# New weights and hand-over delays for the list scheduler of a two-layer attention kernel, and its weight products put under the scheduler

## The chip, the cores and the metric

The kernel runs on one core of one Trainium2 chip. The metric is device time in microseconds (us): the time of one execution of the whole program on that core. A second number, the span, comes from the profiler: from the first to the last instruction of one profiled execution. The core has five engines that work side by side, each through its own list of instructions in a fixed order: TensorE (PE in the profile, with PEld for its weight loads), VectorE (DVE), ScalarE (ACT), GpSimd (POOL) and SyncE (SP, which here only starts transfers). An instruction waits on semaphores for what it needs; while it waits, everything behind it on its engine waits too.

## What is computed

The input x has 8 batches of 64 x 16 positions with 128 channels, so 1024 tokens per batch. There are two layers.

```
# layer 0, per batch: 8 heads over all 1024 tokens
scores = einsum('bhlfc,bhmgc->bhlfmg', q, k) / sqrt(128)
a = softmax(scores, axis=4)          # over m (64)
a = softmax(a, axis=5)               # over g (16)
z1 = layernorm(a @ v @ wo + bo + x)
y  = layernorm(relu(z1 @ w1 + b1) @ w2 + b2 + z1)

# layer 1, per batch
Wi = einsum('bnd,ed->bne', norm(y), W)
s[i,j] = sum_d v[d] * tanh(Wi[j,d] + Wi[i,d])      # 1024 x 1024 x 128 tanh values
y = y + softmax(s, axis=-1) @ norm(y)
# then a recurrence over the 1024 tokens: y_t = sigmoid(wx_t + y_(t-1) @ V), added to y
```

The matrix s is symmetric, so the kernel computes a little more than half of it: some 4.2 million tanh values in each of the 128 partitions.

## The kernel before

**Weights are folded.** For each of the 8 heads the kernel multiplies wq with wk (tile A) and wv with wo (tile Wvo), each 128 x 128, and works out two bias vectors, ub and zb. In the kernel before, this is written out ahead of the scheduled part (lines 775 to 793): all of A and Wvo in turn on PE (L779) with copies by DVE (L782), then ub (L788, L789), with zb (L792, L793) between, and a small mask `half` (L749 to L754). The four weight tensors are loaded into the first four stretches of 1024 elements of the big tile `th`; xT, the transposed tokens, is loaded by SP right behind the first of them.

**Then a planner writes the order.** Everything from the first head of batch 0 to the last row of layer 1 of batch 7 is not written in order; it is added to a `Plan`. Each entry names an engine (or several to choose from), an estimated duration in us, the keys that it reads and writes, and a due time `pri`. `Plan.emit` then simulates the engines: an entry becomes ready when what it depends on has ended and a delay has passed, and that delay depends on the engine that ran it (`LATENCY`, or `AGAIN` when the next one is on the same engine). At each step the entry with the earliest due time among those that can start within 0.15 us of the earliest start is emitted. So durations and delays never reach the chip; they decide the order of each engine's list, and, where an entry has a choice, the engine.

**Layer 0** (function `layer0`), per head and per tile of 128 queries: u = A x + ub (PE L909, eviction L913 or L915), values (L923, L865 or L867), scores (PE L948, 16 matmuls on 32-column strips), exp (ACT L956), sums over m (PE L965, DVE L970), reciprocal (DVE L977), spreading over the partitions (PE L982), division (DVE L990). Two such tiles make a pair: second exp (ACT L1024), sums over g (DVE L1027), reciprocal (DVE L1030), division (POOL L1039), transposes (DVE L1042), attention times values (PE L1050), adding up in `zs` (DVE L1056, L1058). Then come a layer norm, the feed-forward part (L1098, L1102/L1104, L1112 to L1120) and another norm (L814, L815, L818, L819, L824), with affine steps on POOL (L1131, L1132).

**Layer 1** (function `group`): for some rows i of s, four interleaved columns c at a time, the sum Wi[j] + Wi[i] and its tanh are needed over all j. There are three ways:

- ACT alone: tanh of wiT with Wi[i] as the bias, one instruction per row (L1164, "direct");
- POOL adds the rows of a column in one instruction (L1174), and ACT later takes the tanh of all the group's added rows in one wide instruction (L1222);
- DVE adds, row by row with `tensor_scalar` and an accumulator that nobody reads (L1168), or, where a group has four or more rows, with one `tensor_tensor` (also L1174); the wide tanh follows too.

Which of them a group gets is the planner's choice, by which engine can start first. PE multiplies the rows with v into the PSUM tile `sa` (L1242), ACT takes the exp (L1338), POOL and DVE finish the diagonal block (L1344, L1348), and PE does the attention (L1371). The added rows lie in `th`, used as a ring: a POOL or DVE row can start only when PE has used up the rows that lay there.

**Interleaving**: layer 0 of batch b + 1 is planned beside layer 1 of batch b. Layer 0 of batch 0 has nothing beside it, and layer 1 of batch 7 has only the end of layer 0 of batch 7. After the plan come the normalisation over all batches, the recurrence (L1540 to L1561) and the output (L1570, L1572).

```
    LATENCY = {"PE": 0.6, "ACT": 0.5, "DVE": 0.4, "POOL": 0.6, "SP": 8.0}
    AGAIN = {"PE": 0.0, "ACT": 0.0, "DVE": 0.2, "POOL": 0.15, "SP": 8.0}
...
        def ready_at(n, e):
            t = max((began[d] for d in ops[n][7]), default=0.0)
            for d in ops[n][4]:
                t = max(t, done[d] + (self.AGAIN if by[d] == e else self.LATENCY).get(by[d], 0.0))
            return t
```

Of the kernel before, what the change touches and what calls it, by code (L numbers as in the profile page):

```python
# [15 lines left out]
P = 128  # L16
# [466 lines left out]
class Plan:  # L483
# [15 lines left out]
    LATENCY = {"PE": 0.6, "ACT": 0.5, "DVE": 0.4, "POOL": 0.6, "SP": 8.0}  # L499
# [134 lines left out]
def fast_path(ctx: ExitStack, tc: tile.TileContext, a: dict, fits):  # L634
# [79 lines left out]
    wkn = early(1, "wkn", nc.scalar)  # L714
    nc.sync.dma_start(out=xTs[0], in_=a["xt"][0])
    wvn = early(2, "wvn", nc.scalar)
    wo = early(3, "wo", nc.sync)
    bq = load(const, "bq", [P, H], nc.scalar)
# [21 lines left out]
    def by_token(x):  # L740
        return x.rearrange("p (r c) -> p c r", c=4)
# [6 lines left out]
    upper, moved = E_sb[:, 0, :], E_sb[:, 1, :]  # L748
    make_upper_triangular(nc, upper)  # L749
    nc.vector.scalar_tensor_tensor(upper, ident, -0.5, upper, ALU.mult, ALU.add)  # L750
    nc.vector.tensor_copy(half.rearrange("p (c r) -> p c r", c=4), by_token(upper))
    nc.vector.tensor_copy(moved.rearrange("p (c r) -> p c r", c=4), by_token(ident))
    nc.tensor.matmul(m0[:, :P], moved, half, start=True, stop=True)
    nc.vector.tensor_copy(half, m0[:, :P])  # L754
# [22 lines left out]
    for dst, left, right, pp in ((A, wqn, wkn, scs[0]), (Wvo, wvn, wo, scs[1])):  # L777
        for h in range(H):
            nc.tensor.matmul(pp[:, h * C : (h + 1) * C], left[:, h, :], right[:, h, :], start=True, stop=True)  # L779
            if h % 4 == 3:  # L780
                hs = slice(h - 3, h + 1)
                nc.vector.tensor_copy(  # L782
                    dst[:, hs, :], pp[:, (h - 3) * C : (h + 1) * C].rearrange("p (h c) -> p h c", c=C)
                )

    ub = tile_of(const, "ub", [P, H])
    for h in range(H):
        nc.tensor.matmul(m0[:, h : h + 1], wkn[:, h, :], bq[:, h : h + 1], start=True, stop=True)  # L788
    nc.vector.tensor_copy(ub, m0[:, :H])  # L789
    zb = tile_of(const, "zb", [P, 1])  # L790
    for h in range(H):
        nc.tensor.matmul(m1[:, 0:1], wo[:, h, :], bvn[:, h : h + 1], start=h == 0, stop=h == H - 1)  # L792
    nc.vector.scalar_tensor_tensor(zb, m1[:, 0:1], float(M), bo, ALU.mult, ALU.add)  # L793
# [10 lines left out]
    def layer_norm(src, kr, dst, kw, k, pri, on="POOL", then=None):  # L804
# [27 lines left out]
        add(("DVE", 1.9), statistics, r=[kr], w=[ks], pri=pri)  # L832
        add(("POOL", 1.5), power, r=[ks], w=[ks], pri=pri)
        add((on, 1.1 if on == "DVE" else 2.2), normalise, r=[kr, ks], w=kw, pri=pri, give=then)
# [24 lines left out]
    def copy(dst):  # L859
        def fn(e, bank):  # L860
            src = bank
            if len(dst.shape) == 3:
                src = bank[:, : dst.shape[1] * P].rearrange("p (t c) -> p t c", c=P)
            if e == "ACT":
                nc.scalar.activation(dst, src, AF.Copy)  # L865
            else:
                nc.vector.tensor_copy(dst, src)  # L867

        return fn

# [3 lines left out]
    def layer0(b):  # L874
# [17 lines left out]
        for n_part, part in enumerate(parts):  # L892
# [3 lines left out]
            for h in range(H):  # L896
# [8 lines left out]
                for s in range(2) if part is None else (part,):  # L905
# [11 lines left out]
                    through_bank(project, 0.9, [kx], biased, evict(0.75), [], [("u", h % 2, s)], L0, banks)  # L917
                for s in () if alone and n_part else range(2):

                    def values(bank, h=h, s=s):  # L920
# [7 lines left out]
                        values, 0.95, [kx], copy(vp[:, 4 * s : 4 * s + 4, :]), evict(0.68), [], [kvp + (s,)], L0, banks  # L928
                    )
                for qt in qts:  # L930
# [24 lines left out]
                    add(("PE", 1.74), scores, r=[kx, ("u", h % 2, qt // 4)], w=[kc], pri=L0, mode="groups")  # L955
                    add(("ACT", 0.98), lambda _, sc=sc, source=source: nc.scalar.activation(source, sc, AF.Exp, scale=SCALE),  # L956
                        r=[kc], w=[ksrc], pri=L0)
                    if by_pe:
# [15 lines left out]
                        through_bank(sums, 0.45, [ke], last_sums, ("DVE", 0.2), [], [k1], L0, banks, "groups")  # L974
# [17 lines left out]
                        add(("DVE", 0.2), first_inverse, r=[k1], w=[k1], pri=L0)  # L992
                        through_bank(spread, 0.3, [k1], divide, ("DVE", 1.22), [ke], [ke], L0, banks, "groups")
# [30 lines left out]
                    add(("ACT", 1.9), lambda _, e2=e2: nc.scalar.activation(e2, e2, AF.Exp), r=ks, w=ks, pri=L0)  # L1024
# [8 lines left out]
                    add(("DVE", 0.9), second_inverse, r=[k2], w=[k2], pri=L0)  # L1033
                    for q in range(2):
# [6 lines left out]
                        add(("POOL", 1.97), divide_again, r=[ke, k2], w=[ke], pri=L0)  # L1041
                        add(("DVE", 1.17), lambda _, e=e: nc.vector.transpose(e, e), r=[ke], w=[ke], pri=L0)  # L1042
# [17 lines left out]
                    for s in range(2):  # L1060
                        add(
                            ("PE", 1.74), lambda _, attend=attend, s=s: attend(s),
# [3 lines left out]
                    add(("DVE", 0.42), gather, r=[("bank", bank), kx], w=[kz + (qt // 4,)], pri=L0, give=bank)  # L1066

            L0 = b - 1 - SOON
            for qh in range(2) if part is None else (part,):
# [8 lines left out]
                add(("PE", 0.52), lambda _, bank=bank, z_tiles=z_tiles: z_tiles(bank()), r=[kz + (qh,)], w=[kb], pri=L0,  # L1078
# [4 lines left out]
                def affine1(e, bank, z1T=z1T):  # L1083
# [6 lines left out]
                    transposes([Xg[:, i, :] for i in range(4)]), 0.52, [kg], affine1, evict(0.75), [], [k1], L0, banks  # L1090
# [4 lines left out]
                for f in range(NFF):  # L1095
# [10 lines left out]
                    through_bank(hidden, 0.9, [k1], relu, evict(0.75), [], [kh[f]] if f % 2 == 0 else [kh[f]], L0, banks)  # L1106
# [20 lines left out]
                add(("PE", 5.4), outer, r=kh + [k1], w=[kb], pri=L0, take=bank, wait=[kg])  # L1127
# [6 lines left out]
                add(("POOL", 2.2), affine2, r=[kg], w=[kg], pri=L0)  # L1134
# [510 lines left out]
```

## Time and profile before

| what | value |
|---|---|
| median of 3 runs | 5300.66 us (5299.17 to 5303.35) |
| the profiled execution | 5300.69 us |
| its span | 5298.8 us |
| mean granted TensorE clock | 0.987 |
| instructions | 184474 |
| first tanh on ACT (L1164) | starts at 294.5 us |
| last exp on ACT (L1338) | starts at 5207.4 us |

The views used are: the page (busy time of each engine, the chain of work that ended last, the costliest groups), the table of busy time in stretches of the span, the groups by line, the timeline of one engine in a window, and the list of waits. In a group, "x1544" is the number of instructions and "mean ns" the mean recorded duration. Recorded durations of neighbours on one engine overlap a little, so where an exact price is wanted, it is taken from one start to the next. A PE matmul of the program shows as two instructions in the counts (x32 for the 16 matmuls of one score tile).

### The profile page before, as it was taken

The numbers are of one execution on the slowest core, as the hardware profiler recorded it, in microseconds if no ns is written. First come the engines' busy times: TensorE is split into PE (matmuls) and PEld (weight loads), VectorE is DVE, ScalarE is ACT, GpSimd is POOL, SyncE is SP. The second block draws the span as 40 slices with busy tenths as digits, with TensorE's granted clock in tenths as the row PEclk, the third lists the DMA queues.
The fourth block names the chain that finished last, engine by engine and source line by source line (L and its number), as shares of the span: only waits on it lengthen the run. The fifth ranks groups of instructions, "written<-read, shape, count | busy, mean of one in ns | idle before, by whom it ended". The sixth has DMA issues, their size and how long they took to land.

```text
span 5298.8 us, 184474 instructions
## 1 busy us (share of the span) xinstructions
PE 4915.6 (93%) x82181; PEld 3021.0 (57%) x82181; DVE 4739.3 (89%) x9090; ACT 4957.7 (94%) x3692; POOL 4437.4 (84%) x3064
## 2 busy tenths in 40 slices
PE   8899999999999999999999999999998999986567
PEld 6666656656665566556655566555664556552125
DVE  5788988889999999989998999989998999999886
ACT  4389999999999999999999999999999999999995
POOL 2366988679999899979999899989998989897992
PEclk9999999999999999999999999999999999998999
DMA  2000000000000000000000000000000000000001
GB/s 64 2 3 7 3 2 6 2 10 3 2 6 8 4 3 6 4 8 2 3 6 6 6 3 2 6 8 4 3 3 2 10 2 2 2 29 9 1 1 69
DMA packets 27669, 43.16 MB, mean 8 GB/s; under 512 B 2512, under 2 KB 19280, under 8 KB 26864
## 3 DMA queue, kind: packets, MB, share of 16 engines
q1 hardware_dynamic: 24832, 27.99, 1.6%
q8 instruction: 645, 10.57, 0.9%
q10 hardware_dynamic: 1872, 3.16, 0.2%
q14 instruction: 160, 1.31, 0.1%
q0 software_dynamic: 160, 0.13, 0.0%
HBM read 19.22 MB, written 12.06 MB: 6 GB/s over the span
## 4 chain that ended last, share of the span: by engine, by line
PE 67%; ACT 15%; DVE 11%; issue 5%; POOL 1%; DMA 0%; SPq 0%; ACTq 0%; DVEq 0%; POOLq 0%
PE sa L1242 23%; PE sc L948 14%; PE m L1050 13%; ACT th L1222 10%; DVE th L1168 3%; PE m L965 3%; ACT th L1164 3%; PE m L923 2%; PE m L982 2%; PE m L1371 2%; DVE stat_e L1027 2%; PE m L909 1%; DVE wx L990 1%; DVE th L1174 1%; PE m L1120 1%
## 5 line engine op out<-in xcount | busy, mean ns | idle before, releaser
L1174 POOL TENSOR_TENSOR th<-wiT 128x1024 f32<-128x1024 f32 (+55 forms) x2254 | 3255.7, 1479 | 308.9 <-PE sa L1242 270.3
L1222 ACT ACTIVATE th<-th 128x3210 f32<-128x3210 f32 (+57 forms) x1074 | 2926.5, 2767 | 27.0 <-DVE th L1174 15.6
L1242 PE MATMUL sa<-th,vpat 128*32 128x512 f32 (+33 forms) x24576 | 2045.9, 460 | 243.4 <-ACT th L1222 222.9
L1168 DVE TENSOR_SCALAR_CACHE_REDUCE th<-wiT 128x344 f32<-128x344 f32 (+61 forms) x2362 | 1945.8, 863 | 79.6 <-PE sa L1242 76.3
L1242 PEld LDWEIGHTS sa<-th,vpat 128*32 128x32 f32 x24576 | 715.7, 110 | 1186.2 <-issue 681.7
L1164 ACT ACTIVATE th<-wiT 128x501 f32<-128x501 f32 (+59 forms) x1544 | 1120.2, 797 | 16.1 <-PE sa L1242 14.9
L948 PE MATMUL sc<-xT,wx 128*32 128x256 f32 x16384 | 980.3, 380 | 2.2 <-issue 2.2
L1039 POOL TENSOR_TENSOR wx<-wx,stat_e 128x1024 f32<-128x1024 f32 x342 | 658.6, 1948 | 242.5 <-DVE stat_e L1030 153.9
L948 PEld LDWEIGHTS sc<-xT,wx 128*32 128x32 f32 x16384 | 549.9, 110 | 291.4 <-issue 45.5
L1050 PE MATMUL m<-wx 128*128 128x256 f32 x2400 | 563.1, 388 | 18.6 <-DVE stat_e L970 7.7
L1050 PEld LDWEIGHTS m<-wx 128*128 128x128 f32 x2400 | 449.6, 192 | 146.2 <-issue 45.6
L990 DVE TENSOR_TENSOR wx<-wx,m 128x1024 f32<-128x1024 f32 x330 | 396.9, 1206 | 38.6 <-PE m L982 36.8
L956 ACT ACTIVATE wx<-sc 128x1024 f32<-128x1024 f32 x342 | 340.3, 1022 | 93.8 <-PE sa L1050 35.9
L1042 DVE STREAM_TRANSPOSE wx<-wx 128x1024 f32<-128x1024 f32 x342 | 417.6, 1230 | 4.1 <-POOL wx L1039 3.6
L1039 POOL TENSOR_TENSOR e<-e,stat_e 128x1024 f32<-128x1024 f32 x170 | 327.1, 1946 | 97.6 <-DVE stat_e L1030 62.4
L1027 DVE TENSOR_REDUCE stat_e<-wx 128x128 f32<-128x2048 f32 x171 | 388.5, 2272 | 17.3 <-ACT wx L1024 16.1
L1024 ACT ACTIVATE wx<-wx 128x2048 f32<-128x2048 f32 x171 | 327.3, 1915 | 30.3 <-DVE wx L990 30.0
L982 PEld LDWEIGHTS m<-stat_e,ident 128*32 128x32 f32 x15808 | 224.0, 111 | 149.9 <-issue 76.7
L1050 PE MATMUL m<-e,wx 128*128 128x256 f32 x1184 | 278.6, 389 | 16.8 <-DVE e L1042 9.8
L1050 PEld LDWEIGHTS m<-e,wx 128*128 128x128 f32 x1184 | 221.7, 192 | 79.4 <-issue 21.7
L982 PE MATMUL m<-stat_e,ident 128*32 128x16 f32 x15808 | 229.2, 185 | 18.7 <-DVE stat_e L977 5.8
L1030 DVE RECIPROCAL stat_e<-stat_e 128x128 f32<-128x128 f32 x256 | 240.0, 938 | 0.2
(215 smaller groups left out, 4801.4 us busy)
## 6 DMA issues: line engine op xcount, KB each, us to landing
xT<-in_xt_dram SPq DMA_DIRECT2D x8, 512.0 KB, 3.4
th<-in_x_dram SPq DMA_DIRECT2D x8, 512.0 KB, 7.1
parked<-X SPq DMA_DIRECT2D x16, 256.0 KB, 2.3
xr<-parked SPq DMA_DIRECT2D x8, 512.0 KB, 6.9
parked_wx<-bT SPq DMA_DIRECT2D x14, 256.0 KB, 2.3
wx<-parked_wx SPq DMA_DIRECT2D x7, 512.0 KB, 3.7
out_dram<-ot ACTq DMA_DIRECT2D x8, 256.0 KB, 2.2
out_dram<-ot SPq DMA_DIRECT2D x8, 256.0 KB, 2.2
```

What stands on the lines that cost most here:

```text
L948: nc.tensor.matmul(sc[32 * a : 32 * a + 32, 256 * s : 256 * s + 256], u[:, rows], tokens[:, a], start=True, stop=True,)
L982: nc.tensor.matmul(bank[32 * a : 32 * a + 32, s * G : s * G + G], ident[:, 32 * s : 32 * s + 32], r1, start=True, stop=True,)
L990: nc.vector.tensor_tensor(quarters(e), quarters(e), r, ALU.mult)
L1027: nc.vector.tensor_reduce(r2, e2.rearrange("p q (m g) -> p q m g", g=G), AX.X, ALU.add)
L1039: nc.gpsimd.tensor_tensor(e3, e3, r2[:, q, :].unsqueeze(2).to_broadcast([P, M, G]), ALU.mult)
L1042: add(("DVE", 1.17), lambda _, e=e: nc.vector.transpose(e, e), r=[ke], w=[ke], pri=L0)
L1050: nc.tensor.matmul(bank()[:, :256], vp[:, t, :], keys[:, t], start=t == 0, stop=t == NT - 1)
L1164: nc.scalar.activation(rows(c)[:, r, :], wiT[:, i0 + begin[c] :], AF.Tanh, bias=w_i(c, r))
L1168: nc.vector.tensor_scalar(rows(c)[:, r, :], wiT[:, i0 + begin[c] :], w_i(c, r), 0.0, ALU.add, ALU.add, accum_out=next_unused())
L1174: eng.tensor_tensor(rows(c), wiT[:, i0 + begin[c] :].unsqueeze(1).to_broadcast(shape), w_i(c).unsqueeze(2).to_broadcast(shape), ALU.add,)
L1222: nc.scalar.activation(slot()[:, a:z], slot()[:, a:z], AF.Tanh)
L1242: nc.tensor.matmul(sa[32 * c : 32 * c + 32, s:s1], vpat[:, 31 - r0 - r : 63 - r0 - r], rows(c)[:, r, s - at0 - begin[c] : s1 - at0 - begin ...
```

## The change

Three things are changed.

1. The hand-over delays of the planner: PE 0.6 to 0.3, ACT 0.5 to 0.25, DVE 0.4 to 0.25, POOL 0.6 to 0.3 us. `AGAIN` stays.
2. The durations of some thirty kinds of entries. Most get smaller, some larger.
3. The weight products, ub, zb and `half` are no longer written out ahead of the plan. A new function adds them to it, in halves of four heads, with due times ahead of layer 0; they go through the PSUM banks m0, m1 and the two halves of sa, where the products had used the two score banks. Entries that use A, Wvo, ub, zb or `half` now name them as keys. The load of bq moves from behind wv to right behind wk on ACT's queue.

```
-    LATENCY = {"PE": 0.6, "ACT": 0.5, "DVE": 0.4, "POOL": 0.6, "SP": 8.0}
+    LATENCY = {"PE": .3, "ACT": .25, "DVE": .25, "POOL": .3, "SP": 8.0}
...
     wkn = early(1, "wkn", nc.scalar)
+    bq = load(const, "bq", [P, H], nc.scalar)
     nc.sync.dma_start(out=xTs[0], in_=a["xt"][0])
     wvn = early(2, "wvn", nc.scalar)
     wo = early(3, "wo", nc.sync)
-    bq = load(const, "bq", [P, H], nc.scalar)
...
-    for dst, left, right, pp in ((A, wqn, wkn, scs[0]), (Wvo, wvn, wo, scs[1])):
-        for h in range(H):
-            nc.tensor.matmul(pp[:, h * C : (h + 1) * C], left[:, h, :], right[:, h, :], start=True, stop=True)
...
+    def folded_weights():
+        first, later = -2.0, -1.36
+        for hs in (slice(0, 4), slice(4, 8)):
+            for name, dst, left, right, keys in (("A", A, wqn, wkn, (0, 1)), ("Wvo", Wvo, wvn, wo, (2, 3))):
+                def product(bank, left=left, right=right, hs=hs):
+                    for i, h in enumerate(range(hs.start, hs.stop)):
+                        nc.tensor.matmul(bank[:, i * C : (i + 1) * C], left[:, h, :], right[:, h, :], start=True, stop=True)
...
+                through_bank(
+                    product, 1.05, [("xn", k) for k in keys], kept, ("DVE", 0.6), [], [(name, hs.start)],
+                    later if hs.start else first if name == "A" else first + 0.6, four,
+                )
...
-        add(("DVE", 1.9), statistics, r=[kr], w=[ks], pri=pri)
-        add(("POOL", 1.5), power, r=[ks], w=[ks], pri=pri)
+        add(("DVE", 1.62), statistics, r=[kr], w=[ks], pri=pri)
+        add(("POOL", 1.27), power, r=[ks], w=[ks], pri=pri)
...
-                    through_bank(project, 0.9, [kx], biased, evict(0.75), [], [("u", h % 2, s)], L0, banks)
+                    through_bank(project, 0.96, [kx, ("A", h // 4 * 4), ("ub", h // 4 * 4)], biased, evict(0.66), [], [("u", h % 2, s)], L0, banks)
...
-                    add(("PE", 1.74), scores, r=[kx, ("u", h % 2, qt // 4)], w=[kc], pri=L0, mode="groups")
-                    add(("ACT", 0.98), lambda _, sc=sc, source=source: nc.scalar.activation(source, sc, AF.Exp, scale=SCALE),
+                    add(("PE", 1.73), scores, r=[kx, ("u", h % 2, qt // 4)], w=[kc], pri=L0, mode="groups")
+                    add(("ACT", 0.91), lambda _, sc=sc, source=source: nc.scalar.activation(source, sc, AF.Exp, scale=SCALE),
...
-                        through_bank(spread, 0.3, [k1], divide, ("DVE", 1.22), [ke], [ke], L0, banks, "groups")
+                        through_bank(spread, 0.28, [k1], divide, ("DVE", 1.13), [ke], [ke], L0, banks, "groups")
...
-                        add(("POOL", 1.97), divide_again, r=[ke, k2], w=[ke], pri=L0)
-                        add(("DVE", 1.17), lambda _, e=e: nc.vector.transpose(e, e), r=[ke], w=[ke], pri=L0)
+                        add(("POOL", 1.9), divide_again, r=[ke, k2], w=[ke], pri=L0)
+                        add(("DVE", 1.15), lambda _, e=e: nc.vector.transpose(e, e), r=[ke], w=[ke], pri=L0)
...
-            "POOL": lambda c: (0.27 + 1.62e-3 * k * (w - begin[c]), lambda: add_rows(nc.gpsimd, c)),
-            "DVE": lambda c: (k * (0.21 + 1.05e-3 * (w - begin[c])), lambda: [add_row(c, r) for r in rows_of])
+            "POOL": lambda c: (0.138 + 1.686e-3 * k * (w - begin[c]), lambda: add_rows(nc.gpsimd, c)),
+            "DVE": lambda c: (k * (0.193 + 0.966e-3 * (w - begin[c])), lambda: [add_row(c, r) for r in rows_of])
             if k < 4
-            else (0.15 + 1.04e-3 * k * (w - begin[c]), lambda: add_rows(nc.vector, c)),
+            else (0.138 + 0.957e-3 * k * (w - begin[c]), lambda: add_rows(nc.vector, c)),
...
-            lambda: ("ACT", sum(0.2 + 0.833e-3 * (z - a) for a, z in filled())) if filled() else None,
+            lambda: ("ACT", sum(0.1 + 0.833e-3 * (z - a) for a, z in filled())) if filled() else None,
```

The direct tanh of ACT keeps its weight, 0.18 + 0.833e-3 per element, and so do the products with v on PE, at 1.69e-3 per element. The kinds of instructions and the values that they compute are the same; what moves is their order, and which engine adds a row of Wi.

## The prediction, on record before the changed kernel ran

> **What bounds the kernel now.** I read the page first, then busy time by stretch, then the groups by line, the waits, and the timelines of ACT, DVE and PE. The page's first part and the stretches:
>
> ```profile
> PE 4915.6 (93%) x82181; PEld 3021.0 (57%) x82181; DVE 4739.3 (89%) x9090; ACT 4957.7 (94%) x3692; POOL 4437.4 (84%) x3064
> ```
>
> ```profile
> core 0: us, PE busy (x) PEld busy (x) DVE busy (x) ACT busy (x) POOL busy (x), PEclk, DMA share, GB/s
> 294.50:5207.40 4912.90, 4588.73 (x76851) 2768.33 (x76843) 4476.74 (x8615) 4808.11 (x3371) 4343.54 (x2995) 0.99 0.02 5
> 0.00:294.50 294.50, 257.02 (x4791) 189.32 (x4791) 205.25 (x313) 121.20 (x225) 90.39 (x64) 0.97 0.11 30
> 5207.40:5298.80 91.40, 69.83 (x547) 63.35 (x547) 57.27 (x164) 28.35 (x98) 3.44 (x6) 0.90 0.27 99
> 700.00:4600.00 3900.00, 3770.84 (x64319) 2331.75 (x64315) 3590.05 (x6798) 3819.04 (x2592) 3504.53 (x2426) 0.99 0.02 5
> ```
>
> 294.5 is the first tanh, 5207.4 the last exp of layer 1. Between them ACT is idle for 4912.9 - 4808.1 = 104.8 us of 4912.9 (2.1%): 81 of it between 700 and 4600, 3.4 behind 4600. That long middle is bound by ACT. PE's 97% is less than it looks: the chain of work prices one score tile at 1.73 us, a pair's attention at 3.65, one set of sums at 0.45; with all kinds counted out this way I get an estimate of some 4500 us where the page shows 4916, so PE has perhaps 8% in hand. The head (294.5 us) is a chain of PE and DVE. The tail (91.4 us) is the recurrence and the output.
>
> Who makes the tanh rows:
>
> ```profile
> L1174 POOL TENSOR_TENSOR th<-wiT 128x1024 f32<-128x1024 f32 (+55 forms) x2254 | 3255.7, 1479 | 308.9 <-PE sa L1242 270.3
> L1222 ACT ACTIVATE th<-th 128x3210 f32<-128x3210 f32 (+57 forms) x1074 | 2926.5, 2767 | 27.0 <-DVE th L1174 15.6
> L1168 DVE TENSOR_SCALAR_CACHE_REDUCE th<-wiT 128x344 f32<-128x344 f32 (+61 forms) x2362 | 1945.8, 863 | 79.6 <-PE sa L1242 76.3
> L1164 ACT ACTIVATE th<-wiT 128x501 f32<-128x501 f32 (+59 forms) x1544 | 1120.2, 797 | 16.1 <-PE sa L1242 14.9
> L1174 DVE TENSOR_TENSOR th<-wiT 128x768 f32<-128x768 f32 (+20 forms) x74 | 116.3, 1615 | 2.4 <-PE sa L1242 2.3
> ```
>
> Every element goes through ACT once, directly (L1164) or after POOL or DVE added it (L1222). What differs is ACT's fixed cost:
>
> ```profile
> 2046.50 0.88 ACT L1164 ACTIVATE th<-wiT 128x668 f32<-128x668 f32 x1
> 2047.24 2.47 ACT L1222 ACTIVATE th<-th 128x2698 f32<-128x2698 f32 x1
> 2049.59 1.04 ACT L956 ACTIVATE wx<-sc 128x1024 f32<-128x1024 f32 x1
> ```
>
> From start to start a direct row of 668 took 0.74 us and a wide one of 2698 took 2.35. At 0.83 ns an element (a wide row of 4096, 3.51 us from start to start, against one of 2280, 2.01) that leaves 0.185 us of overhead for a direct row and 0.11 for a wide instruction.
>
> **The sum, part by part.** The counts are from the two kernels' instruction lists; the prices from rows of before.
>
> *Rows move off ACT.* L1164 goes from 1544 to 1264 instructions, L1222 from 1074 to 1129; their elements together stay at 4,223,936, 177,136 change from direct to wide. ACT: -280 x 0.185 = -51.8 and +55 x 0.11 = +6.0, so **-45.8 us**. (By busy time less elements, 0.227 and 0.177 an instruction, it would be -53.8.) By batch: -224 and +48 in batches 1 to 6 (-36.1), the rest in the first and last. ACT does this work where it is 98 to 100% busy, so I count all of it.
>
> *They land on DVE and POOL.* DVE: +132 rows with 119,508 elements. A row of 1024 takes 1.20 us from start to start and one of 384 takes 0.53, so 0.13 + 1.05 ns an element: 17 + 125 = +142. The four-row adds go from 74 to 87, at 116.3/74 = 1.57 each: +20. POOL: +66 instructions with 52,804 elements, at 3255.7 us for 1,733,960 elements: +99. Nearly all lies between 700 and 4600. After the change that stretch would be 3900 - 36 = 3864 long, with ACT at 3783, DVE at 3590 + 155 = 3745 (97%), POOL at 3504 + 99 = 3604 (93%). The cover is DVE's idle time, 310 us now and 119 then; the price if it is not there is a rival below.
>
> *The order.* The planner's old weights were above what the trace shows, but not on every engine. Old minus new weight times count: DVE some 340 us (L1168 2362 x 0.07 = 167, L990 512 x 0.09 = 46, L970 36, the rest small), against 436 us that DVE idles in the middle; POOL some 220 (2254 x 0.08 + 512 x 0.07) of 569; ACT 169 (1074 x 0.1, 512 x 0.07, 256 x 0.1) of 105. PE's weights hardly change. So most of DVE's idle time is time in which the plan held it busy: it ran ahead and met PE, which was priced right.
>
> ```profile
> DVE zs L1058 <- PE m L1050: 72.6, 89, 3.8
> DVE stat_e L970 <- PE m L965: 35.6, 76, 1.8
> ACT wx L956 <- PE sc L948: 13.0, 21, 1.5
> ACT wx L956 <- PE m L1050: 11.6, 12, 2.4
> ```
>
> These waits (700 to 4600) are what a plan with true weights can fill. The delays don't become too short: in the timeline a DVE division ends at 2054.24 and ACT's second exp starts at 2054.27, and the planned 0.25 counts from about 0.1 before the recorded end. How ACT's idle of 104.8 us changes no row shows. Ends: the share behind 4600 (0.6%) over the whole middle is 27 us, a gain of 78; the share from 294.5 to 700 (20.4 of 405.5, 5%) is 243, a loss of 138. Nearest is the stretch from 1000 to 4000, 42.8 of 3000 or 1.4%, which gives 69; I go about a third of the way there: **-10 us**.
>
> *The products.* PE's list before the first u (L909):
>
> ```profile
> 12.34 2.05 PE L779 MATMUL sc<-th 128*128 128x128 f32 x8 [1.38 <-DMA th<-in_wo_dram]
> 14.18 3.41 PE L792 MATMUL m<-bvn_sb,th 128*128 128x1 f32 x16
> 20.49 3.57 PE L788 MATMUL m<-bq_sb,th 128*128 128x1 f32 x16 [0.55 <-DVE half L754]
> 24.32 2.08 PE L909 MATMUL m<-xT,A 128*128 128x512 f32 x2 [0.26 <-DVE ub L789]
> ```
>
> In the new list all of it still stands ahead of the first u, only `half` is gone: A's first half at 6.02 (2.07), ub's first half (1.8, if bq lands in time), then PE waits for wo until 12.34, then Wvo 2.05, A 2.05, Wvo 2.05, ub 1.8, zb 3.41: u at 23.7 in place of 24.32, **-0.6**. If bq lands as late as now (10.7 us after its issue), ub's first half moves behind 12.3 and u starts at 25.5, +1.2. SP's queue keeps its order; the loads of x behind it now wait for the products' readers, but only the bound check reads x, and nothing on the path waits for that. DVE's copies are the same in number. POOL first needs `half` at the first L1344, near 393 us. In the rest of the head the same 44 first exps, 21 second exps and 64 squares precede ACT's first tanh in both lists; I take 0 there, with -20 to +10, the idle time of PE in it (37 us) being the most there is.
>
> The Trainium skill has a rule against this change ("SBUF — State Buffer", section "Who interferes with whom"): a DVE instruction with two SBUF inputs and a GpSimd instruction that reads SBUF exclude each other for a whole instruction. The trace agrees:
>
> ```profile
> L1174 DVE TENSOR_TENSOR th<-wiT x74: 387/1134/10806, 394.9 to 4858.4; 128x1024 f32<-128x1024 f32 x8, 128x768 f32<-128x768 f32 x5, 128x828 f32<-128x828 f32 x3, 128x700 f32<-128x700 f32 x3
> ```
>
> One such add took 10.8 us. ACT waited 15.6 us for them (L1222's row above); 87 in place of 74 makes that 18.3, by which the sum would be 2.7 higher.
>
> Sum against the profiled execution, 5300.69 (span 5298.8; 1.9 lie around it; the median of the runs is 5300.66): 5300.7 - 45.8 - 10 - 0.6 = **5244 us**.
>
> **The rivals.**
>
> *PE is the bound in the middle*, and ACT's saving turns into waits for PE. For: the chain of work is 67% PE, and ACT's waits above are for PE. Against: PE's estimate above, and DVE and POOL rather than ACT idle most. Then only the first and last batch (-9.6) count, and -0.6: 5290. This is also the case in which the change does not do what it says. Chance 0.15.
>
> *DVE becomes the bound* (the other side). DVE has 3745 us of work between 700 and 4600. If its 310 us of waiting stay, because they are real hand-overs and not plan errors, the stretch takes 4055; the point from which it is slower than now is 3900 - 3745 = 155 us, half of the waits. With two thirds left: 3745 + 207 = 3952, +52, less 10 elsewhere: 5342. Against: 340 of 436 us are accounted for by weights. Chance 0.08.
>
> *The plan fits much better*: ACT's idle falls to the 27 us and the head gains 15: 5300.7 - 46 - 78 - 15 = 5162. For: waits for PE are most of ACT's idle time. Against: between 1000 and 4000 ACT already idles 1.4%. Chance 0.12.
>
> **The numbers.** 5244 has 0.65, for 5205 to 5280. The range 5180 to 5300 takes in that, most of the PE case and the nearer part of the good case. A measurement here tells about 0.2% (10.6 us) from no change. Faster by more than that: 0.65 + 0.12 + half of the PE case = 0.84; within it 0.08; slower 0.08.
>
> **What would show it.** Right: L1164 x1264 and L1222 x1129 with ACT busy near 4907; first tanh near 294; ACT's idle share in the middle at 2% or below; DVE's busy time up by some 160, and less waiting of L1058 and L970 for PE. Wrong: ACT's idle time well over 105 us (then look whether L956 waits for PE, or L1222 for DVE); a first tanh moved by over 10 us; L1168 or L1174 costing more apiece than before.

## The result, and the profile after

The changed kernel takes **5235.91 us** (median of 4 runs, 5231.66 to 5242.02) against 5302.01 for the kernel before in the same comparison (5299.17 to 5304.87): ratio 0.9883, 95% interval 0.9871 to 0.9895, or 62 us. Its profiled execution took 5237.67 us with a span of 5235.8. The sum of the prediction, 5244, is 8 us above it. Its terms are another matter, as the runs below show.

The first part of the page after:

```profile
PE 4889.8 (93%) x82181; PEld 3013.3 (58%) x82181; DVE 4885.7 (93%) x9372; ACT 4907.7 (94%) x3463; POOL 4536.1 (87%) x3130
```

ACT's busy time fell by 50.0 us (from 4957.7, predicted 4907), DVE's rose by 146.4, POOL's by 98.7. The groups of the tanh rows (the lines of the code have moved down by 27: L1164 is now L1191, L1222 L1249, L1168 L1195, L1174 L1201):

```profile
L1249 ACT ACTIVATE th<-th 128x3402 f32<-128x3402 f32 (+55 forms) x1129 | 3080.3, 2773 | 27.4 <-DVE th L1201 15.3
L1195 DVE TENSOR_SCALAR_CACHE_REDUCE th<-wiT 128x840 f32<-128x840 f32 (+60 forms) x2494 | 2088.7, 875 | 64.2 <-PE sa L1269 63.3
L1191 ACT ACTIVATE th<-wiT 128x596 f32<-128x596 f32 (+52 forms) x1264 | 913.1, 792 | 9.2 <-PE sa L1269 9.1
```

The counts are those of the prediction, and an instruction costs about what it cost (L1191 792 ns against 797, L1195 875 against 863, with other lengths in the mix). To see where the time went I cut both executions at the same three events: the first direct tanh, the last scores of layer 0 (L975, before L948), and the last wide tanh to start. Busy time by stretch, after, in the columns of the view shown for before (this is the second and the third stretch), and then the same two of the kernel before:

```profile
272.00:4624.50 4352.50, 4228.19 (x73095) 2636.02 (x73087) 4172.38 (x7856) 4248.52 (x2884) 3998.91 (x2746) 0.99 0.02 5
4624.50:5140.90 516.40, 339.95 (x3748) 125.47 (x3740) 448.53 (x1040) 510.63 (x264) 443.56 (x316) 0.96 0.03 9
```

```profile
294.50:4695.80 4401.30, 4252.88 (x73165) 2643.61 (x73161) 4041.38 (x7613) 4299.90 (x3085) 3915.51 (x2690) 0.99 0.02 5
4695.80:5204.30 508.50, 333.69 (x3662) 123.90 (x3654) 435.36 (x1003) 506.31 (x287) 428.03 (x306) 0.95 0.03 9
```

| stretch | before | after | difference | ACT idle | PE idle | DVE idle |
|---|---|---|---|---|---|---|
| head, to the first direct tanh | 294.5 | 272.0 | -22.5 | | 37.5 to 22.9 | |
| mixed, both layers side by side | 4401.3 | 4352.5 | -48.8 | 101.4 to 104.0 | 148.4 to 124.3 | 359.9 to 180.1 |
| last rows, no layer 0 left | 508.5 | 516.4 | +7.9 | 2.2 to 5.8 | 174.8 to 176.4 | 73.1 to 67.9 |
| end | 94.5 | 94.9 | +0.4 | | | |

(Idle is length less busy.) The head after, beside the prediction's row 0.00:294.50:

```profile
0.00:272.00 272.00, 249.14 (x4783) 187.00 (x4787) 207.51 (x314) 118.22 (x220) 90.14 (x64) 0.98 0.12 33
```

In the mixed stretch, 83% of the time, ACT lost 51.4 us of work and the stretch 48.8 us of length. That looks like a bound by ACT, as forecast. But PE also idles 24 us less, and is busy 25 us less with the same 82,181 instructions in the whole run; which of these is the cause, no view of these two kernels alone can say. The head's gain was not forecast.

### The profile page after: what moved, and what is told of

It is laid out like the page before. It is cut to its first block, busy times and chain, and to the rows that moved or that the text cites. A ratio compares the mean times of both kernels' runs of the same rounds, so it can differ in the third digit from the quotient of the medians.

```text
span 5235.8 us, 184559 instructions
## 1 busy us (share of the span) xinstructions
PE 4889.8 (93%) x82181; PEld 3013.3 (58%) x82181; DVE 4885.7 (93%) x9372; ACT 4907.7 (94%) x3463; POOL 4536.1 (87%) x3130
## 4 chain that ended last, share of the span: by engine, by line
PE 67%; DVE 14%; ACT 12%; issue 5%; POOL 2%; DMA 0%; ACTq 0%; DVEq 0%; POOLq 0%; SPq 0%
PE sa L1269 23%; PE sc L975 13%; PE m L1077 13%; ACT th L1249 9%; DVE th L1195 4%; PE m L992 3%; PE m L950 2%; PE m L1009 2%; PE m L1398 2%; DVE th L1201 2%; ACT th L1191 2%; DVE stat_e L1054 1%; PE m L936 1%; DVE wx L1017 1%; DVE wx L1069 1%
## 5 line engine op out<-in xcount | busy, mean ns | idle before, releaser
L1201 POOL TENSOR_TENSOR th<-wiT 128x798 f32<-128x798 f32 (+58 forms) x2320 | 3355.6, 1482 | 186.9 <-PE sa L1269 175.4
L1249 ACT ACTIVATE th<-th 128x3402 f32<-128x3402 f32 (+55 forms) x1129 | 3080.3, 2773 | 27.4 <-DVE th L1201 15.3
L1269 PE MATMUL sa<-th,vpat 128*32 128x512 f32 (+34 forms) x24576 | 2042.4, 460 | 230.8 <-ACT th L1249 220.1
L1195 DVE TENSOR_SCALAR_CACHE_REDUCE th<-wiT 128x840 f32<-128x840 f32 (+60 forms) x2494 | 2088.7, 875 | 64.2 <-PE sa L1269 63.3
L975 PE MATMUL sc<-xT,wx 128*32 128x256 f32 x16384 | 981.9, 380 | 0.2 <-ACT e L983 0.2
L1191 ACT ACTIVATE th<-wiT 128x596 f32<-128x596 f32 (+52 forms) x1264 | 913.1, 792 | 9.2 <-PE sa L1269 9.1
L975 PEld LDWEIGHTS sc<-xT,wx 128*32 128x32 f32 x16384 | 553.5, 110 | 278.3 <-issue 39.0
L992 PEld LDWEIGHTS m<-wx,same_row 128*32 128x32 f32 x10464 | 188.6, 110 | 90.5 <-issue 41.5
```

What stands on the lines that cost most here:

```text
L975: nc.tensor.matmul(sc[32 * a : 32 * a + 32, 256 * s : 256 * s + 256], u[:, rows], tokens[:, a], start=True, stop=True,)
L992: nc.tensor.matmul(bank[32 * s : 32 * s + 32, 0:64], same_row, e[:, cols], start=i == 0, stop=i == 3)
L1191: nc.scalar.activation(rows(c)[:, r, :], wiT[:, i0 + begin[c] :], AF.Tanh, bias=w_i(c, r))
L1195: nc.vector.tensor_scalar(rows(c)[:, r, :], wiT[:, i0 + begin[c] :], w_i(c, r), 0.0, ALU.add, ALU.add, accum_out=next_unused())
L1201: eng.tensor_tensor(rows(c), wiT[:, i0 + begin[c] :].unsqueeze(1).to_broadcast(shape), w_i(c).unsqueeze(2).to_broadcast(shape), ALU.add,)
L1249: nc.scalar.activation(slot()[:, a:z], slot()[:, a:z], AF.Tanh)
```

## The experiments

Theory A is the prediction's: ACT bounds the middle, and the time follows ACT's work. Its rivals are PE, or DVE, as the bound there, and that the gain is one of order. In the ratios below the kernel before was run on the same chip each time; the changed kernel stands at 0.9883.

### Which part of the change does it

**e1_delays**: the kernel before with the new delays alone.

```
-    LATENCY = {"PE": 0.6, "ACT": 0.5, "DVE": 0.4, "POOL": 0.6, "SP": 8.0}
+    LATENCY = {"PE": .3, "ACT": .25, "DVE": .25, "POOL": .3, "SP": 8.0}
```

> The kernel before with the shorter hand-over delays alone (durations and prelude as before). In its program the direct tanh rows on ACT are 1428 (before 1544, after 1264) and the wide ones 1104 (1074, 1129), so ACT's fixed cost by the rates of the prediction, 0.185 and 0.11 us, falls by 18 us instead of 46. But 3367 matmuls stand ahead of the first product of a row instead of 2596: at 0.11 us a matmul (270 us of the old head by its 2596) the first row starts some 80 us later, and ACT has only 34,816 more elements (about 33 us) to do in that time. Theory (the time is ACT's busy time and its idle time, most of it before the first row): 5302 - 18 + 47 = about 5330 us, slower than before. Rival (shorter delays by themselves make a closer-fitting order): below 5290 us.

Measured 5322.7 us, ratio 1.0037 (1.0023 to 1.0051): slower, as expected. First direct tanh at 368.0 (expected near 375). ACT's busy time fell by only 4.7, not 18.

**e2_weights**: the new durations alone (every edited number inside an `add`, `through_bank` or `work` entry).

```
-        add(("DVE", 1.9), statistics, r=[kr], w=[ks], pri=pri)
+        add(("DVE", 1.62), statistics, r=[kr], w=[ks], pri=pri)
...
-            lambda: ("ACT", sum(0.2 + 0.833e-3 * (z - a) for a, z in filled())) if filled() else None,
+            lambda: ("ACT", sum(0.1 + 0.833e-3 * (z - a) for a, z in filled())) if filled() else None,
```

> The changed durations alone (old delays, products ahead of the plan as before). Direct rows 1396, wide 1105: fixed cost of ACT 24 us less than before. 2806 matmuls ahead of the first row product (before 2596): the first row some 22 us later, of which ACT fills about 9. Theory (ACT's busy time plus its idle time before the first row): 5302 - 24 + 13 = about 5291 us. Rival (the time goes with DVE's and POOL's loads, as DVE has 97 us more of row adds by 0.13 us + 1.05 ns an element): 5302 or above.

Measured 5279.8 us, ratio 0.9955 (0.9941 to 0.9968): 24 us faster by the ratio, 13 more than the theory allowed. First direct tanh at 320.2.

**e4_both**: delays and durations, with the products ahead of the plan as in the kernel before.

```
-    folded_weights()
```

> The changed kernel with its products written out ahead of the plan as before: delays and durations together, without the third part. Direct rows 1324, wide 1119: ACT's fixed cost 36 us below before and 10 above after; 2436 matmuls ahead of the first row product (after: 2444). Theory: the rest of the head (from the first u to the first row) has the 17.5 us gain already, the first u has not (24.3 us); so 5236 + 10 + 5 = about 5251 us, and the first direct row near 277 us. Rival (the head's gain is the products' being planned): first direct row near 290 us, time about 5263.

Measured 5256.6 us, ratio 0.9913 (0.9899 to 0.9926); first direct tanh at 277.1, where the theory had 277 and the rival 290. So the parts don't add. Delays alone cost 20 us, durations alone bring 24, both together bring 46. With either alone more of layer 0 is planned ahead of the first row (3367 and 2806 matmuls, against 2436 with both). The planned products bring the last 16 us (0.9913 to 0.9883); in the two profiled executions the head is 5.1 us shorter, the mixed stretch 6.3 and the last rows 5.1. The planner also shares the rows out differently there (1324 to 1264 direct); what that did to the latter two was not tried by itself.

### Is ACT the bound?

**s_split**: the changed kernel in the same order, with more ACT instructions for the same elements.

```
-                nc.scalar.activation(slot()[:, a:z], slot()[:, a:z], AF.Tanh)
+                m = a + (z - a) // 2 if g % 2 else z
+                nc.scalar.activation(slot()[:, a:m], slot()[:, a:m], AF.Tanh)
+                if m < z:
+                    nc.scalar.activation(slot()[:, m:z], slot()[:, m:z], AF.Tanh)
```

> The changed kernel, same order, with the wide tanh of every second group emitted as two instructions of half the length: 562 more ACT instructions and not one element more. Theory (ACT bounds the middle): each costs its fixed 0.11 us, so 562 x 0.11 = 62 us, time about 5297 us. Rival (PE bounds the middle): ACT has 111 us of idle time there, the time stays within 10 us of 5236. Rival (DVE bounds it): about the same as for PE, with ACT's waits for DVE shrinking.

Measured 5252.9 us, ratio 0.99 (0.9885 to 0.9915). By the medians that is 17 us slower than the changed kernel, by the ratios, which compare on the same chip, 9 us with overlapping intervals: far from the 62 of the theory, and at or somewhat above the rivals' 10. The timeline of ACT confirms the price of an instruction (start, duration; L1250 and L1252 are the two halves):

```profile
2008.15 1.34 ACT L1250 ACTIVATE th<-th 128x1373 f32<-128x1373 f32 x1
2009.39 1.34 ACT L1252 ACTIVATE th<-th 128x1373 f32<-128x1373 f32 x1
2010.63 0.87 ACT L1191 ACTIVATE th<-wiT 128x691 f32<-128x691 f32 x1
```

From start to start 1.24 us for 1373 elements, of which 1.14 are elements: 0.10 us fixed. The Trainium skill ("ScalarE: Activation LUTs", section "What ACT_TABLE_LOAD costs") gives about 186 ns fixed for an ACTIVATE with immediates, 93 more for a bias that is a column, and an overlap of about 93 between neighbours; an estimate from these figures is 93 and 186 back to back. The trace agrees with both (0.10 here; in the changed kernel seven direct rows of 664 take 5.17 us from the first start to the next instruction's, 0.74 each, of which 0.55 are elements: 0.19). ACT's busy time rose by 47.1 (4954.8), and is again almost that of the kernel before (4957.7). Yet the time rose by only 9 to 17. **With the old kernel's load on ACT, the new order is still 46 us faster** (span 5252.9 against 5298.8; 53 by the ratio), 23.1 us of them in the head. So 30 us or more of the 47 went into time in which ACT had waited. Its mixed stretch:

```profile
271.40:4634.80 4363.40, 4257.44 (x73097) 2652.75 (x73090) 4161.64 (x7856) 4287.00 (x3358) 4001.82 (x2746) 1.00 0.02 5
```

ACT has only 12.9 us less to do here than in the mixed stretch of the kernel before, and the stretch is 37.9 us shorter: some 25 us of that must have another source than ACT's load.

**rel_a, rel_d, rel_ad**: the changed kernel in the same order, with work taken away from ACT, from DVE, and from both (what is left out is named in the expectations).

```
-                    add(("ACT", 1.8), lambda _, e2=e2: nc.scalar.activation(e2, e2, AF.Exp), r=ks, w=ks, pri=L0)
+                    add(("ACT", 1.8), lambda _, e2=e2: nc.scalar.activation(e2[:, :, 0:768], e2[:, :, 0:768], AF.Exp), r=ks, w=ks, pri=L0)
...
-                        nc.vector.reciprocal(r2, r2)
+                        nc.vector.reciprocal(r2[:, 0, :], r2[:, 0, :])
```

> The changed kernel, same order, with the second exponential on 768 of every 1024 elements only (the others keep the first result; this part of the computation is left out): 512 x 0.833 ns x 256 = 109 us less work on ACT, none less elsewhere. Theory A (ACT bounds): 5236 - 109 = about 5127 us. Theory E (ACT, DVE and PE bound together): adding 47 us to ACT cost 17, so taking away can give at most that rate, 39 us, and less the more is taken: 5197 to 5236 us. Theory C (DVE alone): within 5 us of 5236.

> The changed kernel, same order, with the second reciprocals done for one of the two halves only (64 of 128 elements a partition); the other half's sums stay uninverted, so this part of the computation is left out. By the rows of the reciprocals (0.94 us for 128 elements, 0.23 for 16, so about 0.54 for 64) DVE has some 103 us less to do, no other engine less or more. Theory C (on the changed kernel's side DVE bounds: the time is DVE's busy time plus about 350 us of idle): 5236 - 103 + what ACT then bounds, at most the 22 us by which its line, busy plus 328, could lie lower: anything clearly below 5225 us. Theory E (ACT, DVE and PE bound together: each has about its smallest idle time of all runs): 5220 to 5240 us, since ACT's work is as before. Theory A (ACT alone): within 5 us of 5236.

> Both of the cuts in the two kernels before: ACT 109 us and DVE 103 us less, same order, both parts of the computation left out. Theory of two bounds (ACT and DVE, PE merely waits for them): about 100 us less, 5136 us. Theory E (PE bounds with them: its middle is 97% busy, and 31 us more of its work cost 23): not over 40 us less, above 5196 us. If the cuts alone gave a and d, and they add (each engine's work lies on the path in places of its own): 5236 - a - d.

Measured: 5242.4 us, ratio 0.9891 (0.9875 to 0.9907); 5253.3, 0.9899 (0.9884 to 0.9914); 5243.0, 0.9884 (0.9869 to 0.99). **No gain from any of them.** ACT's busy time was 90 us lower, DVE's 62 (not 109 and 103), and the time did not fall. The mixed stretch of rel_ad, then its chain of work and that of the changed kernel:

```profile
267.30:4629.60 4362.30, 4230.77 (x73107) 2646.63 (x73103) 4118.20 (x7855) 4166.57 (x2884) 3992.06 (x2745) 0.99 0.02 5
```

```profile
PE 74%; DVE 10%; ACT 8%; issue 4%; POOL 3%; DMA 0%; ACTq 0%; DVEq 0%; POOLq 0%; SPq 0%
```

```profile
PE 67%; DVE 14%; ACT 12%; issue 5%; POOL 2%; DMA 0%; ACTq 0%; DVEq 0%; POOLq 0%; SPq 0%
```

Beside the changed kernel's stretch: ACT 4166.6 instead of 4248.5, DVE 4118.2 instead of 4172.4, the length 4362.3 instead of 4352.5. PE's busy time is the same, 4230.8, and PE's idle time too (131.5 instead of 124.3). ACT's idle time has risen from 104.0 to 195.7: what was saved there became waiting. The chain, 67% PE in the changed kernel, is now 74% PE and only 8% ACT. That ends theory A for the changed kernel. The three runs rule out DVE alone as well.

**p_tax**: the changed kernel, same order, a few products of PE issued twice. **d_tax**: one tiny DVE instruction more in each of 512 places.

```
-                            for s in range(4):
+                            for s in (0, 0, 1, 2, 3):
```

```
                             nc.vector.reciprocal(r1, s1)
+                            nc.vector.memset(next_unused(), 0.0)
```

> The changed kernel, same order, with one quarter of the spreading products issued twice (same result written again): 4 of 16 products in each of 512 groups. Their row (236 us for all) makes that 59 us of PE's time at most, by the planner's 0.28 us a group 36. Theory A (ACT bounds the middle): within 10 us of the changed kernel, 5236 to 5250 us. Theory B (balanced): +12 to +21 us. Theory D (PE is the bound): +36 to +59, 5276 to 5299.

> The changed kernel, same order, with one tiny write of DVE (128x1) after each of the 512 first reciprocals. The nearest rows are the accumulator read of 0.08 us and the reciprocal of 128x1 of 0.15 us, so DVE gets 42 to 79 us more work and no other engine any. Theory A (ACT bounds the middle, DVE has 123 us of idle time between 677 and 4540): within 10 us of the changed kernel, 5236 to 5250 us. Theory B (the middle is balanced: splitting ACT's instructions gave it 47 us and cost 17, so each engine's work is worth about a third): +15 to +28 us, 5251 to 5268. Theory C (DVE is the bound now): +42 to +79, 5278 to 5315.

p_tax: 5256.0 us, ratio 0.9926 (0.9913 to 0.9939), 23 us slower than the changed kernel. d_tax: 5247.2 (5227.5 to 5251.5), 0.9904 (0.9886 to 0.9921). Their mixed stretches, p_tax first:

```profile
274.10:4650.00 4375.90, 4255.67 (x76824) 2672.74 (x76816) 4181.13 (x7856) 4253.30 (x2885) 3998.06 (x2746) 0.99 0.02 5
```

```profile
271.40:4622.40 4351.00, 4229.52 (x73099) 2640.13 (x73091) 4194.93 (x8322) 4248.74 (x2884) 3998.07 (x2746) 0.99 0.02 5
```

PE got 27.5 us of work and the stretch 23.4 of length, 0.85 for one. The same rate for ACT is 0.28 (s_split: 38.5 and 10.9), and for DVE nil (22.6 and -1.5). These rates set one execution against one, and they are rough: the profiled execution of p_tax is the longest of its five (5262.6 us), that of d_tax (5231.9) lies 15 us below its median. By the ratios of all runs p_tax cost 23 us for 31 of PE's work, s_split 9 for 47 of ACT's and d_tax 11 for 18 of DVE's, each give or take some 10. DVE's nil is therefore not shown. Its tax came out smaller than planned, 18 us in the run instead of 42 to 79, and its interval does not tell theories A and B apart. PE's total of 31 lies below the 36 to 59 of the expectation, and its 23 us just above theory B's range. The repeated products also stand in the way of the division that waits for them, so p_tax makes that chain longer as well as PE's work; the two were not told apart.

### Does a plan with still less on ACT win?

Three kernels in which the planner gets another price:

```
-            "ACT": lambda c: (k * (0.18 + 0.833e-3 * (w - begin[c])), lambda: [tanh_row(c, r) for r in rows_of]),
+            "ACT": lambda c: (k * (0.35 + 0.833e-3 * (w - begin[c])), lambda: [tanh_row(c, r) for r in rows_of]),
```

> The changed kernel with the planned price of a direct tanh row raised from 0.18 to 0.35 us, which pushes the same shift further: 1008 direct and 1182 wide rows (after: 1264, 1129), fixed cost of ACT 41 us less by 0.185 and 0.11, DVE's row adds 98 us more by 0.13 us + 1.05 ns an element, POOL's 134 us more. Theory A (ACT bounds): 5236 - 41 = about 5195 us. Theory B (balanced; a third of ACT's saving is worth it, and DVE's and POOL's work costs a third): -14 + 33 and more, 5245 to 5300. Theory C (DVE is the bound): 5236 + 98 - 0 to 30 = above 5300.

```
-            lambda: ("ACT", sum(0.1 + 0.833e-3 * (z - a) for a, z in filled())) if filled() else None,
+            lambda: ("ACT", sum(0.2 + 0.833e-3 * (z - a) for a, z in filled())) if filled() else None,
```

> The changed kernel with one planned duration put back: the fixed part of the wide tanh at 0.2 us instead of 0.1. Its program has fewer direct rows, not more (1176 direct, 1156 wide), 13 us less fixed cost on ACT, 48 us more row adds on DVE and 70 on POOL. Theory A (ACT bounds): about 5222 us. Theory B (balanced): 5236 - 5 + 16 = about 5247. Theory C: above 5270. If below 5236, the measured value was not what helped.

```
-            "POOL": lambda c: (0.138 + 1.686e-3 * k * (w - begin[c]), lambda: add_rows(nc.gpsimd, c)),
+            "POOL": lambda c: (0.138 + 1.55e-3 * k * (w - begin[c]), lambda: add_rows(nc.gpsimd, c)),
```

> The changed kernel with POOL's planned price of a row add lowered from 1.686 to 1.55 us per thousand elements, so that the plan gives POOL more: its program has 1204 direct and 1146 wide rows, ACT's fixed cost 9 us less, DVE's row adds 65 us less, POOL's 160 us more. Theory E without POOL (POOL has 232 us of idle time between 677 and 4540): about 5220 to 5230 us, the best so far. Rival (POOL bounds too: its idle time over the whole run has been 665 to 710 us in all kernels since the changed one): 4536 + 160 + 690 = about 5385 us.

Measured: dr_035 5343.5 us, ratio 1.0088 (1.0074 to 1.0102); w_wide02 5298.0, 0.9995 (0.9986 to 1.0003); q_155 5437.3, 1.0255 (1.0241 to 1.0269). All three have fewer direct rows than the changed kernel, and all are slower than it: by the ratios 109, 59 and 197 us of 5302. **One constant put back, the wide tanh at 0.2 instead of 0.1, gives up the whole gain**, though its program has still fewer direct rows than the changed kernel. The mixed stretches of w_wide02 and q_155:

```profile
272.20:4681.80 4409.60, 4242.89 (x72995) 2640.36 (x72987) 4217.50 (x7990) 4243.39 (x2821) 4029.83 (x2785) 0.99 0.02 5
```

```profile
271.10:4820.50 4549.40, 4291.49 (x73246) 2648.45 (x73238) 4229.37 (x7827) 4277.15 (x2844) 4118.24 (x2850) 0.98 0.02 5
```

In w_wide02 ACT has 5 us less to do than in the changed kernel (4243.4), PE 15 more, and the stretch is 57 us longer: PE idles 166.7 us instead of 124.3, ACT 166.2 instead of 104.0. In q_155 PE idles 257.9, ACT 272.2, DVE 320.0, POOL 431.2: each more than in the changed kernel, so none of them is full. Of the 197 us by which this stretch is longer, 134 are idle time of PE; the other 63 are PE's busy time, for nearly the same number of instructions, at a mean granted clock of 0.975 over the run instead of 0.989. POOL's part shows in q_155's chain of work and in ACT's waits between 677 and 4540:

```profile
PE 46%; POOL 20%; DVE 16%; ACT 10%; issue 8%; DMA 0%; POOLq 0%; ACTq 0%; DVEq 0%
```

```profile
ACT wx L1051 <- DVE wx L1017: 59.2, 19, 11.4
ACT th L1249 <- POOL th L1201: 54.1, 81, 3.4
```

The plan that believes POOL faster than it is queues rows there that come late; ACT waited 54.1 us for them, and 5.6 in the changed kernel. So the rival of q_155 had the direction and too small a number (5385), and its reason, a full POOL, is not what the row shows. In the same way dr_035 lands where theory C had it. In the changed kernel's order rel_d speaks against DVE's work as the reason; in the order of dr_035 that was not tried.

## Why the prediction was right, and where its reasons failed

The total held and the split into terms did not: as far as the runs can tell, too much for the rows was made up by too little for the order and the head. That the sum came within 8 us is luck to that extent. Against the profiled executions (5300.69 to 5237.67, -63.0):

| term | predicted | the runs show |
|---|---|---|
| rows off ACT | -45.8 | about -9 to -17: what the same load costs when it is put back (s_split) |
| order in the middle | -10 | about -23 to -31: the rest, not measured by itself |
| products, first u | -0.6 | -5.0 |
| rest of the head | 0 | -17.5 |

**Rows off ACT.** The mechanism's first half was right: 1264 and 1129 instructions, 0.185 and about 0.1 us fixed, ACT's busy time 50 lower. The step that failed is "ACT does this work where it is 98 to 100% busy, so I count all of it". A share of 98% did not make ACT the bound: in the changed kernel, 90 us less of its work are worth nothing, and 47 more cost 9 to 17. The Trainium skill ("Perfetto Trace Analysis", section "Identifying the Most-Contended Engine") has much the same rule: the engine with the highest occupancy is the one to optimise first, but PE is to be judged by its weight loads and its share of peak instead of its busy share. The trace disagrees here: in the mixed stretch ACT was 97.6% busy, DVE 95.9%, and PE's weight loads took 60.6% (its busy share was 97.1%), so the rule would name ACT, and ACT was not the bound. The number for the rows has a limit: s_split puts the load back in other places than those from which it was taken, and at the new order. What 47 us of ACT's work were worth in the kernel before was not run. The stretch's own differences (-51.4 and -48.8) would allow nearly all of it.

**PE as a rival.** It got 0.15 and the price of 5290. As a mechanism for the changed kernel it was the nearest to right: the step "PE has perhaps 8% in hand" failed. The estimate priced a score tile at 1.73 us; in the page of before the 512 tiles have 980.3 us of busy time, 1.91 each. For the other kinds the runs do not show where it fell short.

```profile
L948 PE MATMUL sc<-xT,wx 128*32 128x256 f32 x16384 | 980.3, 380 | 2.2 <-issue 2.2
```

What PE idles in the mixed stretch, 106 to 141 us in all kernels that share the changed kernel's order, stayed there when ACT and DVE were relieved. Whether PE's own speed or the hand-overs through PE hold it there is not told apart. The price of 5290 left PE's own waits as they were, but PE's idle time over the run fell from 383.2 to 346.0 and its busy time by 25.8. The latter must be read with care: s_split and the changed kernel have the same 82,181 PE instructions, and 4966.4 and 4889.8 us of busy time. The Trainium skill ("Perfetto Trace Analysis", section "Tensor Engine Instruction (MATMUL, LD_WEIGHTS)") says that the ends of PE's instructions are modelled. No run shows whether that is where the 76.6 us come from.

**Order.** The forecast that DVE would wait less for PE held. These are DVE's waits after, between 700 and 4600:

```profile
DVE zs L1085 <- PE m L1077: 26.8, 43, 3.1
...
DVE stat_e L997 <- PE m L992: 9.0, 24, 1.0
```

They were 72.6 and 35.6. DVE's idle time in the mixed stretch halved. But the size was put on ACT's idle time, which did not fall (104.8 to 111.0 by the prediction's own cut). PE's fell by 24.1 in the mixed stretch; that the order gained by way of it is likely by rel_ad and p_tax, but was not shown for the kernel before. "A third of the way" to the 69 us of the nearest stretch had no row behind it. The waits of L1249 for DVE's four-row adds, which one paragraph of the prediction feared for, stayed at 15.3 us (15.6 before), with 87 adds in place of 74. The add of 10.8 us named there (the median is 1.1) ran from 4512.94 to 4523.75; beside it POOL did eight of its adds without a break, from 4513.15 to 4523.14.

**The head.** This is the term put at nothing, "I take 0 there", because the same ACT instructions precede the first tanh; it measured -17.5, inside the -20 to +10 given for it. PE's list is the same too: 4791 PE instructions in the counts ran ahead of the first direct tanh before, 4783 after. What shrank between the first u and that tanh is PE's waiting, from 28.5 to 14.9 us; its busy time fell by 4.0. A first tanh moved by over 10 us was one of the prediction's own signs of being wrong, and it came (22.5). The count in e4_both's expectation (2436 matmuls against 2596) is of those ahead of the first product of a row, which started 17.1 us after the first tanh before and 6.0 us after it in e4_both. So e4_both met its 277 us for another reason than the one given: 4760 PE instructions ran ahead of its first tanh, and PE waited 27.3 us in its head instead of 37.5. Of the 5.0 us at the first u (19.35 instead of 24.32), 3.9 are PE's busy time, at prices which the prediction took as constant. PE's timeline after:

```profile
11.88 3.79 PE L855 MATMUL sa<-th 128*128 128x128 f32 x16 [0.91 <-DMA th<-in_wvn_dram]
15.46 1.45 PE L855 MATMUL m<-th 128*128 128x128 f32 x8
16.75 0.95 PE L866 MATMUL m<-bq_sb,th 128*128 128x1 f32 x8
17.56 1.93 PE L875 MATMUL sa<-bvn_sb,th 128*128 128x1 f32 x16
```

**DVE as the bound** did not come: it worked 180.1 us short of the mixed stretch, and its idle time fell as argued, from 310 to 125 us between 700 and 4600. **What stays open**: which hand-overs hold PE's last 124 us, what bound the kernel before, and why neighbouring plans lose 59 to 197 us; q_155 shows POOL's late rows, for w_wide02 no single wait stands out. That POOL shares the bound in the changed kernel was not tried; no run takes work from POOL alone.

## What to carry to other kernels

When several engines are each over 95% busy, the busiest is not thereby the bound: take work away from it in the same order, and see whether the time moves, before counting a saving in full. A list scheduler's weights are worth measuring as a set: here durations alone gave 24 us, delays alone lost 20, both gave 46, and a single wrong constant lost all of it again. Look at the engine that feeds a stage's first instruction, at its list and at its waits, and not only at the engine that waits: with 6439 and 5307 PE instructions ahead of the first direct tanh it came at 368.0 and 320.2 us (e1_delays, e2_weights), with 4791 and 4783 at 294.5 and 272.0.

## What the runs showed of the hardware

The same products of PE did not always take the same time. Four products of 128x128 (x8 in the counts) took 2.08 us at 5.93 and 1.45 at 15.46, after PE had run without a break from 11.88, for 3.6 us; eight of 128x1 (x16) took 3.41 in the kernel before, where they started 1.8 us behind the end of a pause of PE, and 1.93 here. The view by stretch gives a granted clock of 1.00 for all these places, so that column does not show it. The Trainium skill ("TensorE: Matmul & The Clock Gate", section "What's actually happening") has PE at half its clock until it has been busy for about 3.4 us. The trace agrees only in part: the times fell to 0.70 and 0.57, and in the kernel before PE ran without a break from 12.34, and four products still took 2.06 us 5.1 us later:

```profile
17.45 2.06 PE L779 MATMUL sc<-th 128*128 128x128 f32 x8
```

So 3.6 us of work is not a threshold that these runs establish, and what makes PE faster stays open here.
